# A convolution and a GRU on one core: x chunk 1 loaded behind the weights, candidate products by input part over a seeded bank, W_hh loaded gate by gate

## The chip, the core and the metric

The kernel runs on one core of one Trainium2 chip, in float32. The time is that of one execution on the device, in microseconds; the time of a kernel is the median of its runs. The profile is one more execution, recorded by the hardware profiler.

## The reference

The input x has 16 batch rows, 256 steps and 512 channels. First a causal depthwise convolution over time with 16 taps (the conditioning matrix gives one tap for each of its 16 rows), added to x. Then a GRU over the 256 steps, whose start state is the conditioning matrix, added to its own input:

```python
def _L0_cond_ref(x, w):                     # w: (16, 1, 512), K = 16
    return jax.lax.conv_general_dilated(x, w, window_strides=(1,), padding=[(K - 1, 0)],
        dimension_numbers=('NHC', 'HIO', 'NHC'), feature_group_count=C)

def cell(h, x):                             # W_ih, W_hh: (512, 1536); gates r, z, n
    gi = x @ W_ih + b_ih
    gh = h @ W_hh + b_hh
    i_r, i_z, i_n = jnp.split(gi, 3, axis=-1)
    h_r, h_z, h_n = jnp.split(gh, 3, axis=-1)
    r = jax.nn.sigmoid(i_r + h_r)
    z = jax.nn.sigmoid(i_z + h_z)
    n = jnp.tanh(i_n + r * h_n)
    h_new = (1.0 - z) * n + z * h
    return (h_new, h_new)

x = x + _L0_cond_ref(x, cond_2048[:, None, :])
x = x + _L1_cond_ref(cond_2048, x, W_ih, W_hh, b_ih, b_hh)
```

## The kernel before

**Layout.** The 512 channels lie on 128 partitions in four input parts, q (or kc) = 0 to 3. The 256 steps are cut into 16 chunks of 16 steps. A chunk of x arrives in `x_nat` by eight transfers (L125), VectorE transposes it into `xT` in two pieces (`turn`, L219), and the 16 steps before it are copied in front as a halo (ScalarE, L215). The convolved chunk is `x1T`. ScalarE makes the first term of each part (`first`, L236); the other 15 taps of each part are VectorE instructions that add to `x1T` in place (L257): 60 taps a chunk. `tap_units` gives their order: tap number k outside, part q inside.

**A step of the GRU** (`step`). TensorE multiplies the state with W_hh for r, then n, then z (`recurrent`, L409, 16 products each; the profile counts two instructions for one float32 product). The products add to PSUM banks that already hold the biases (`seed_rz` and `seed_nh`, copies on ScalarE) and, for r and z, the products of x with W_ih (`pair_units`, L374, a pair of steps at a time). The x part of the candidate comes from `ni_units` (L311): blocks of NI = 8 steps, for each output part q four input parts kc; when one q is complete it is evicted to SBUF with its bias added (L323), which makes four evictions a block. After sigmoid of r (ScalarE, L426), VectorE does `rn` (L435), its transpose (L437), `n` (L439), the transpose of z's products (L448), the difference `dn` (L454) and two halves of a scan that gives the new state (L461). `seen` (L389) is a copy of one element, a glance, with which VectorE takes note that ScalarE is done. Each engine runs its instructions in the order of the program, which is written by hand (`manual_schedule`).

**Work between.** `bulk_work` is called in each step after r's products are issued, and so lies on VectorE before `rn`. It draws one output unit (`out_units`: `sum` L497 or `store` L509, the sum and the transposition of 8 steps, two units in 8 steps) if one is due, then units of the `Plan`: taps, halos, transpositions. A unit has a cost (0.402 us a tap, 0.7 a transposition) and a due step. The quota of a step is `bulk.rate(t) + 0.175`, where `rate` is the greatest sum of costs up to a unit, divided by the steps left until it is due. Units are given while the sum plus half of the next cost is within the quota and the sum stays within ROOM = 2.05; a unit that is due in the next step is given in any case. Taps of chunk c were due 8 steps before the chunk begins. `other_products` gives, behind the step's own products on TensorE, up to two units of the next pair and two of the next candidate block.

**The start.** TensorE marks its banks (`mark`) and runs PAD tiny products to warm up. Chunk 0's parts 2 and 3 are convolved on TensorE with diagonal matrices (`conv_on_tensor`, L284; the diagonals from ScalarE, L280), parts 0 and 1 by taps on VectorE. Then the biases are spread by TensorE (`spread_biases`, L353), and the candidate's block 0 and the first pair are computed. Before step 0 the plan may give 10 us of chunk 1's taps (`bulk.run(0, HEAD)`, L582).

**Transfers.** SP and POOL issue the loads in the order of the program: the conditioning, x chunk 0, x chunk 1, the biases, then W_ih and W_hh in four transfers each (`load_weights`, L170, two on SP's queue, two on POOL's), then x chunk 2. A transfer on a queue waits until the one issued eight before it has landed.

Of the kernel before, what the change touches and what calls it, by code (L numbers as in the profile page):

```python
# [24 lines left out]
F32 = mybir.dt.float32  # L25
# [7 lines left out]
GT = 8  # L33
R, Z, N = 0, 1, 2
CHUNKS = (16,) * 16
PAD = 111
HEAD = 10.0
SYNC = mybir.DependencyInfo(mybir.DependencyClass.Sync, mybir.DependencyReason.DATA)
Q_PE = (2, 3)
NI = 8  # L40
# [35 lines left out]
def conv_gru_kernel(  # L76
# [29 lines left out]
    op = ctx.enter_context(tc.tile_pool(name="op", bufs=3))  # L106
    dram = ctx.enter_context(tc.tile_pool(name="dram", bufs=1, space=bass.MemoryType.DRAM))
    ps = ctx.enter_context(tc.tile_pool(name="ps", bufs=1, space=PSUM))
    ps_ni = ctx.enter_context(tc.tile_pool(name="ps_ni", bufs=2, space=PSUM))

    ctx.enter_context(tc.manual_schedule())

# [20 lines left out]

    warm = const.tile([P, 1], F32)
    nc.vector.memset(warm, 0.0)
    blank = const.tile([P, 2 * P], BF16)
    nc.vector.memset(blank, 0.0)
    for j in range(NQ):
        (nc.sync, nc.scalar)[j % 2].dma_start(
# [11 lines left out]
    nc.vector.memset(ones, 1.0)  # L151
    bn_nat = const.tile([P, P], F32)
    nc.vector.memset(bn_nat, 0.0)

    load_x(1, ((nc.sync,), (nc.gpsimd,)))
    nc.sync.dma_start(out=b_two[0:1, :], in_=b_hh.rearrange("(o c) -> o c", o=1))
    nc.sync.dma_start(
        out=b_two[1:2, 0 : 2 * C], in_=b_ih[0 : 2 * C].rearrange("(o c) -> o c", o=1)
# [5 lines left out]
    wih = const.tile([P, NQ, 3 * C], F32)  # L164
    whh = const.tile([P, NQ, 3 * C], F32)

    def load_weights(w_sb, w):

        for j in (0, 2, 1, 3):
            (nc.sync if j < 2 else nc.gpsimd).dma_start(  # L170
                out=w_sb[L * j : L * j + L],
                in_=w[j * P : (j + 1) * P].rearrange("(q l) c -> l q c", l=L),
            )

    load_weights(wih, w_ih)
    load_weights(whh, w_hh)
    load_x(2)
    zero_z = [const.tile([P, NQ * B * 2], F32, name=f"zero_z_{i}") for i in range(2)]
    for t in zero_z:
# [8 lines left out]
        nc.vector.tensor_scalar_add(last1, condT[:, :, K - 1], 1.0)  # L188

    bnT = const.tile([P, NQ, L], F32)  # L190

    b_rows = const.tile([P, 3, P], F32)

# [52 lines left out]
    def give_firsts(most=99):  # L246
        for _ in range(min(most, len(firsts))):
            firsts.pop(0)[2]()

    def tap_units(c):  # L250

        n = CHUNKS[c] * B

        def tap(k, q):
            while any(item[:2] == (c, q) for item in firsts):
                firsts.pop(0)[2]()
            nc.vector.scalar_tensor_tensor(  # L257
                out=x1T[c][:, q, 0:n],
                in0=xT[c][:, q, k * B : k * B + n],
                scalar=condT[:, q, k : k + 1],  # L260
                in1=x1T[c][:, q, 0:n],
                op0=ALU.mult,
                op1=ALU.add,
            )

        return [
            (0.135 + n / 960.0, lambda k=k, q=q: tap(k, q)) for k in range(K - 1) for q in range(NQ)
        ]

    def conv_on_tensor():  # L270

        n = CHUNKS[0] * B
        diag = const.tile([P, len(Q_PE), K, P], F32)

        def weight(k, q):
            return condT[:, q, k : k + 1] if k < K - 1 else last1[:, q : q + 1]

        for i, q in enumerate(Q_PE):
            for k in range(K):
                nc.scalar.activation(diag[:, i, k], ident, AF.Copy, scale=weight(k, q))  # L280
        for i, q in enumerate(Q_PE):
            acc = ps_ni.tile([P, CHUNKS[0] * B], F32, tag="pni", name=f"conv_{q}")
            for k in range(K):
                nc.tensor.matmul(  # L284
                    acc[:, 0:n],
                    lhsT=diag[:, i, k],
                    rhs=xT[0][:, q, k * B : k * B + n],
                    start=(k == 0),
                    stop=(k == K - 1),
                )  # L290
            evictions.append(lambda q=q, acc=acc: nc.scalar.copy(x1T[0][:, q, 0:n], acc[:, 0:n]))


    blocks = [(t0, NI) for t0 in range(0, T, NI)]

    def ni_units(t0, steps):

        n = steps * B
        c, o = chunk_of(t0)
        units = []  # L300
        hold = {}

        def prod(q, kc):
            if q == 0 and kc == 0:
                hold["ni"] = nip.tile([P, NQ, NI * B], F32, tag="ni", name=f"ni_{t0}")
                for i in range(steps):
                    ni[t0 + i] = hold["ni"][:, :, i * B : (i + 1) * B]
            if kc == 0:
                hold[q] = ps_ni.tile([P, NI * B], F32, tag="pni", name=f"pni_{t0}_{q}")
            for j in range(NQ):  # L310
                nc.tensor.matmul(  # L311
                    hold[q][32 * j : 32 * j + 32, 0:n],
                    lhsT=wih[:, kc, N * C + j * P + q * L : N * C + j * P + q * L + L],
                    rhs=x1T[c][:, kc, o : o + n],
                    start=(kc == 0),
                    stop=(kc == NQ - 1),
                    skip_group_check=True,
                )
            if kc == NQ - 1:
                evictions.append(lambda: evict(q))  # L320

        def evict(q):
            nc.scalar.activation(  # L323
                hold["ni"][:, q, 0:n], hold[q][:, 0:n], AF.Identity, bias=bnT[:, q, 0:1]
            )

        for q in range(NQ):
            for kc in range(NQ):
                units.append(lambda q=q, kc=kc: prod(q, kc))
        return units  # L330

    rz = [ps.tile([P, 2, P], F32, name=f"prz_{i}") for i in range(2)]
    nh = [ps.tile([P, P], F32, name=f"pnh_{i}") for i in range(2)]
    spare = ps.tile([P, 3, P], F32, name="spare")

    def mark():

        for i in range(2):  # L340
            nc.tensor.matmul(rz[i], lhsT=blank[:, 0:P], rhs=blank, start=True, stop=True)
            nc.tensor.matmul(nh[i], lhsT=blank[:, 0:P], rhs=blank[:, 0:P], start=True, stop=True)

    def idle_products(n):

        for _ in range(n):
            nc.tensor.matmul(
                spare[0:L, 0, 0:1], lhsT=blank[:, 0:L], rhs=blank[:, 0:1], start=True, stop=True
            )

    def spread_biases():
        for j in range(NQ):
            nc.tensor.matmul(  # L353
                spare[L * j : L * j + L],
                lhsT=ones,
                rhs=b_two.rearrange("o (g j c) -> o j g c", g=3, j=NQ)[:, j],
                start=True,
                stop=True,
            )

    def seed_rz(p):
        nc.scalar.copy(rz[p % 2], b_rows[:, 0:N])  # L362

    def seed_nh(p):
        nc.scalar.copy(nh[p % 2], b_rows[:, N])
# [28 lines left out]
    def step(t, h, bulk_work, other_products):  # L394
# [34 lines left out]
            tc.add_manual_dep(of_r.ins, of_z[-1].ins.name, SYNC, reason="its own earlier writes")  # L429
        if p + 1 < T // 2:  # L430
            (seed_nh if s else seed_rz)(p + 1)
        recurrent(pnh, N)
        seen(r, 0)
        rn = ew.tile([P, P], F32, tag="rn", name=f"rn_{t}")
# [91 lines left out]
    bulk = Plan()  # L526
    mark()
    idle_products(PAD)
    nc.tensor.drain()
    (_, halo), *turns = turn_units(0)  # L530
    halo()
    for t in hist:
# [12 lines left out]
            )  # L545
    conv_on_tensor()
    for i, (_, fn) in enumerate(tap_units(0)):
        if i % NQ not in Q_PE:
            fn()
    nc.vector.transpose(bnT, by_part(bn_nat))  # L550
    for _, fn in turn_units(1):
        fn()
    evictions.pop(0)()
    first_terms(1)
    give_firsts()
    evictions.pop(0)()
    spread_biases()
    nc.scalar.copy(b_rows, spare)
    seed_rz(0)
    seed_nh(0)  # L560
    for fn in ni_units(*blocks[0]):
        while evictions:
            evictions.pop(0)()
        fn()
    while evictions:
        evictions.pop(0)()
    for fn in pair_units(0):
        fn()
    for c in range(1, NCH):
        due = starts[c] - NI  # L570
        taps = tap_units(c)

        ahead = []
        if c + 1 < NCH:
            ahead = turn_units(c + 1) + [(0.0, lambda c=c: first_terms(c + 1))]
        at = len(taps) - AHEAD
        for cost, fn in taps[:at] + (ahead if c > 1 else []) + taps[at:]:
            bulk.add(cost, due, fn)
        if c == 1:
            for cost, fn in ahead:  # L580
                bulk.add(cost, due + GT // 2, fn)
    bulk.run(0, HEAD)  # L582

    h = (lambda kc: condT[:, kc, 0:B], condT[:, :, 0:B])
    late = []
# [1 line left out]
    for t in range(T):  # L587
        p, s = divmod(t, 2)
        if s == 0 and p + 1 < T // 2:
            of_pair = pair_units(p + 1)  # L590
        if t % NI == 0 and t + NI < T:
            of_block = ni_units(*blocks[t // NI + 1])

        def other_products():

            for units in (of_pair, of_block):
                for _ in range(2):
                    if units:
                        units.pop(0)()

        def bulk_work():

            quota = bulk.rate(t) + 2 * 0.7 / GT
            room = ROOM
            while late and (t >= T - 2 or room == ROOM):
                cost, fn = late.pop(0)
                fn()
                quota -= cost
                room -= cost
            bulk.run(t, quota, room)  # L610

        h = step(t, h, bulk_work, other_products)
        if t == T - 3:
            late += out_units(NG - 1, 0, GP - 1)
        elif t % GT == GT - 1 and t < T - 1:
            late += out_units(t // GT)
        elif t == T - 2:
            late += out_units(NG - 1, GP - 1, GP, (0,))
# [30 lines left out]
```

## Time and profile before

| | |
|---|---|
| runs | 1045.07, 1047.57, 1050.63 us |
| median | 1047.57 us |
| the profiled execution, its own time | 1048.66 us |
| its span, first to last instruction | 1046.7 us |
| busy: TensorE, its weight loads, VectorE, ScalarE | 98%, 88%, 88%, 36% of the span |
| first product of step 0 | 36.87 us |
| first product of step 1 | 42.09 us |
| W_ih landed (first, last of four) | 16.9, 24.1 us |
| W_hh landed (first, last of four) | 28.4, 36.4 us |

In the views of the profile a row names the engine, the line, the operation, the tile written and the tiles read, and the shape. PE is TensorE, PEld its weight load, DVE VectorE, ACT ScalarE, POOL GpSimd, SP the queue that issues transfers. "x5" means that five instructions in a row are merged into one row; the length then runs from the start of the first to the end of the last. In square brackets stands how long the engine sat idle before, and what ended that.

### The profile page before, as it was taken

The page shows a single profiled execution, that of the slowest core. Times are in us where ns is not written, and L with a number is a line of the kernel's source. Part 1 is how long each engine was busy: PE and PEld are TensorE (multiplying, and loading weights), DVE is VectorE, ACT ScalarE, POOL GpSimd, SP SyncE. Part 2 cuts the span into 40 slices and gives each one's busy share as a digit, 9 for nine tenths or more (in the row PEclk, how much of TensorE's full clock was granted, in tenths as well). Part 3 has the DMA queues.
Part 4 walks back from the last instruction along what each step waited for, and adds up shares of the span by engine and source line. Part 5 has one row for each costly group of instructions (what it writes and reads, how often), then busy time and mean ns, then how long its engine had stood idle before and what let it go on. Part 6 is the DMA issues. An engine that isn't in the chain of part 4 may idle for free.

```text
span 1046.7 us, 71583 instructions
## 1 busy us (share of the span) xinstructions
PE 1027.5 (98%) x32955; PEld 919.2 (88%) x32955; DVE 923.5 (88%) x3351; ACT 381.8 (36%) x1520; POOL 8.1 (1%) x21
## 2 busy tenths in 40 slices
PE   7799999999999999999999999999999999999997
PEld 6689989988989988988988988988888988988986
DVE  7899999999999998999999999998999999896555
ACT  5243433334333343333334333343333334333332
POOL 3000000000000000000000000000000000000000
PEclk9999999999999999999999999999999999999999
DMA  9510100101010010100100010010000000000000
GB/s 213 133 28 11 35 15 14 35 12 27 15 29 19 15 33 6 35 15 14 35 13 25 15 32 17 14 33 7 14 15 14 15 13 6 14 14 15 14 13 15
DMA packets 39760, 27.70 MB, mean 26 GB/s; under 512 B 6494, under 2 KB 38306, under 8 KB 39460
## 3 DMA queue, kind: packets, MB, share of 16 engines
q1 hardware_dynamic: 38180, 19.30, 8.4%
q8 instruction: 257, 4.21, 1.7%
q0 software_dynamic: 864, 3.67, 1.5%
q14 instruction: 43, 0.35, 0.1%
q10 hardware_dynamic: 416, 0.16, 0.1%
HBM read 14.73 MB, written 8.39 MB: 22 GB/s over the span
## 4 chain that ended last, share of the span: by engine, by line
PE 94%; DMA 3%; DVE 1%; ACT 0%; issue 0%; SPq 0%; ACTq 0%
PE prz L409 42%; PE pnh L409 21%; PE prz L374 20%; PE pni L311 10%; DMA whh<-in_L_cond_W_hh_dram 3%; DMA x_nat<-in_x_dram 0%; DVE rnT L437 0%; DVE rn L435 0%; DVE zp L448 0%; DVE n L439 0%; ACT zero_z L452 0%; DVE hist L461 0%; SPq L170 0%; DMA out_dram<-o 0%; DVE glance L389 0%
## 5 line engine op out<-in xcount | busy, mean ns | idle before, releaser
L409 PE MATMUL prz<-whh,hist 128*32 128x128 f32 x16320 | 539.2, 273 | 2.6 <-DVE hist L461 2.4
L409 PEld LDWEIGHTS prz<-whh,hist 128*32 128x32 f32 x16320 | 434.0, 103 | 19.5 <-DVE hist L461 5.8
L257 DVE SCALAR_TENSOR_TENSOR x1T<-xT,condT,x1T 128x256 f32<-128x256 f32 x930 | 381.0, 464 | 1.2 <-ACT x1T L236 1.2
L409 PE MATMUL pnh<-whh,hist 128*32 128x128 f32 x8160 | 269.5, 273 | 0.0
L374 PE MATMUL prz<-wih,x1T 128*32 128x256 f32 x4096 | 267.7, 379 | 0.0
L409 PEld LDWEIGHTS pnh<-whh,hist 128*32 128x32 f32 x8160 | 226.4, 104 | 0.0
L446 ACT ACTIVATE dn<-n 128x64 f32<-128x64 f32 x256 | 68.0, 266 | 322.2 <-DVE n L439 322.2
L374 PEld LDWEIGHTS prz<-wih,x1T 128*32 128x32 f32 x4096 | 127.7, 110 | 44.2
L311 PEld LDWEIGHTS pni<-x1T,wih 128*32 128x32 f32 x4096 | 122.1, 110 | 43.2 <-ACT x1T L236 0.6
L426 ACT ACTIVATE r<-prz 128x128 f32<-128x128 f32 x256 | 70.9, 277 | 243.2 <-PE prz L409 240.4
L311 PE MATMUL pni<-x1T,wih 128*32 128x128 f32 x4096 | 157.4, 273 | 0.0
L461 DVE TENSOR_TENSOR_SCAN hist<-zero_z,dn 128x64 f32<-128x64 f32 x512 | 115.4, 261 | 0.0
L435 DVE TENSOR_TENSOR rn<-r,pnh 128x128 f32<-128x128 f32 x256 | 72.8, 284 | 45.7 <-PE pnh L409 42.9
L452 ACT ACTIVATE zero_z<-zp 128x32 f32<-128x32 f32 x512 | 90.7, 226 | 7.6 <-DVE zp L448 0.2
L437 DVE STREAM_TRANSPOSE rnT<-rn 128x128 f32<-128x128 f32 x256 | 79.7, 311 | 8.8
L448 DVE STREAM_TRANSPOSE zp<-prz 128x128 f32<-128x128 f32 x256 | 81.1, 317 | 0.2
L323 ACT ACTIVATE ni<-pni,bnT 128x128 f32<-128x128 f32 x128 | 47.0, 367 | 75.1 <-PE pni L311 75.1
L454 DVE TENSOR_TENSOR dn<-hist,dn 128x64 f32<-128x64 f32 x255 | 58.2, 228 | 9.5
L439 DVE TENSOR_TENSOR n<-rnT,ni 128x64 f32<-128x64 f32 x256 | 57.6, 225 | 8.9
L389 DVE COPY glance<-r 1x1 f32<-1x1 f32 x256 | 34.1, 133 | 29.8 <-ACT r L426 29.6
L362 ACT COPY prz<-b_rows 128x256 f32<-128x256 f32 x128 | 48.6, 379 | 0.0
L389 DVE COPY glance<-zero_z 1x1 f32<-1x1 f32 x256 | 36.3, 142 | 8.9 <-ACT zero_z L452 0.2
(51 smaller groups left out, 216.3 us busy)
## 6 DMA issues: line engine op xcount, KB each, us to landing
out_dram<-o SPq DMA_DIRECT2D x248, 32.0 KB, 2.7
x_nat<-in_x_dram SPq DMA_DIRECT2D x118, 64.0 KB, 3.3
wih<-in_L_cond_W_ih_dram POOLq DMA_DIRECT2D x2, 768.0 KB, 12.8
wih<-in_L_cond_W_ih_dram SPq DMA_DIRECT2D x2, 768.0 KB, 13.9
whh<-in_L_cond_W_hh_dram POOLq DMA_DIRECT2D x2, 768.0 KB, 22.4
whh<-in_L_cond_W_hh_dram SPq DMA_DIRECT2D x2, 768.0 KB, 24.5
x_nat<-in_x_dram POOLq DMA_DIRECT2D x8, 64.0 KB, 5.5
out_dram<-o SPq DMA_DIRECT2D x8, 24.0 KB, 1.6
```

What stands on the lines that cost most here:

```text
L257: nc.vector.scalar_tensor_tensor(out=x1T[c][:, q, 0:n], in0=xT[c][:, q, k * B : k * B + n], scalar=condT[:, q, k : k + 1], in1=x1T[c][:, q ...
L311: nc.tensor.matmul(hold[q][32 * j : 32 * j + 32, 0:n], lhsT=wih[:, kc, N * C + j * P + q * L : N * C + j * P + q * L + L], rhs=x1T[c][:, k ...
L374: nc.tensor.matmul(rz[p % 2][32 * j : 32 * j + 32], lhsT=x1T[c][:, kc, o : o + PAIR], rhs=w_rz[:, :, j * P : (j + 1) * P], start=False, st ...
L389: nc.vector.tensor_copy(glances[i][0:1], of_scalar[0:1, 0:1])
L409: product = nc.tensor.matmul(dst[32 * j : 32 * j + m], lhsT=h[0](kc), rhs=whh[:, kc, g * C + j * P : g * C + (j + 1) * P], start=False, st ...
L426: of_r = nc.scalar.activation(r, pr, AF.Sigmoid)
L435: nc.vector.tensor_mul(rn, r, pnh)
L437: nc.vector.transpose(rnT, by_part(rn))
L446: nc.scalar.activation(dn_v[:, :, :, 1], n, AF.Tanh)
L448: nc.vector.transpose(zp, by_part(pz))
L452: nc.scalar.activation(z_v[:, qs, :, 1], zp[:, qs, half], AF.Sigmoid) for qs in halves
L461: nc.vector.tensor_tensor_scan(hist_g[:, lo + at : lo + at + W // 2], z[:, to], dn[:, to], 0.0, op0=ALU.mult, op1=ALU.add,)
```

## The change

- **Loads.** W_hh comes in twelve transfers, r first, then n, then z, each a 128-row quarter and 512 columns. x chunk 1 comes behind them.
- **Candidate products.** They go by input part: for each kc all four q. A block has one bank of 512 columns (`pni`), which ScalarE fills with the bias beforehand (`seed_ni`, from `bn_rows`); two evictions of 256 columns follow. The convolution of chunk 0 uses two `spare` banks, the first of which `spread_biases` writes later.
- **Taps.** Part q is now outside, tap number k inside, for chunk 0 as well. The taps of part i of chunk c are due at its first step - 7 + 2i.
- **Plan.** Chunk 1's transposition and first terms move from the start into the plan. Nothing is given before step 1 (FIRST). The next chunk's transposition stays 10 taps before the end of a chunk's taps, except for chunk 2, behind all taps of chunk 1.
- **Start.** 108 warming products in place of 111, two more marking products, no drain.

```diff
@@ -33,8 +33,8 @@
 GT = 8
 R, Z, N = 0, 1, 2
 CHUNKS = (16,) * 16
-PAD = 111
-HEAD = 10.0
+PAD = 108
+FIRST = 1
 SYNC = mybir.DependencyInfo(mybir.DependencyClass.Sync, mybir.DependencyReason.DATA)
 Q_PE = (2, 3)
 NI = 8
@@ -106,7 +106,6 @@
     op = ctx.enter_context(tc.tile_pool(name="op", bufs=3))
     dram = ctx.enter_context(tc.tile_pool(name="dram", bufs=1, space=bass.MemoryType.DRAM))
     ps = ctx.enter_context(tc.tile_pool(name="ps", bufs=1, space=PSUM))
-    ps_ni = ctx.enter_context(tc.tile_pool(name="ps_ni", bufs=2, space=PSUM))
 
     ctx.enter_context(tc.manual_schedule())
 
@@ -133,7 +132,7 @@
 
     warm = const.tile([P, 1], F32)
     nc.vector.memset(warm, 0.0)
-    blank = const.tile([P, 2 * P], BF16)
+    blank = const.tile([P, 4 * P], BF16)
     nc.vector.memset(blank, 0.0)
     for j in range(NQ):
         (nc.sync, nc.scalar)[j % 2].dma_start(
@@ -151,8 +150,6 @@
     nc.vector.memset(ones, 1.0)
     bn_nat = const.tile([P, P], F32)
     nc.vector.memset(bn_nat, 0.0)
-
-    load_x(1, ((nc.sync,), (nc.gpsimd,)))
     nc.sync.dma_start(out=b_two[0:1, :], in_=b_hh.rearrange("(o c) -> o c", o=1))
     nc.sync.dma_start(
         out=b_two[1:2, 0 : 2 * C], in_=b_ih[0 : 2 * C].rearrange("(o c) -> o c", o=1)
@@ -164,16 +161,18 @@
     wih = const.tile([P, NQ, 3 * C], F32)
     whh = const.tile([P, NQ, 3 * C], F32)
 
-    def load_weights(w_sb, w):
+    def load_weights(w_sb, w, columns):
 
         for j in (0, 2, 1, 3):
             (nc.sync if j < 2 else nc.gpsimd).dma_start(
-                out=w_sb[L * j : L * j + L],
-                in_=w[j * P : (j + 1) * P].rearrange("(q l) c -> l q c", l=L),
-            )
-
-    load_weights(wih, w_ih)
-    load_weights(whh, w_hh)
+                out=w_sb[L * j : L * j + L, :, columns],
+                in_=w[j * P : (j + 1) * P, columns].rearrange("(q l) c -> l q c", l=L),
+            )
+
+    load_weights(wih, w_ih, slice(0, 3 * C))
+    for g in (R, N, Z):
+        load_weights(whh, w_hh, slice(g * C, (g + 1) * C))
+    load_x(1, ((nc.sync,), (nc.gpsimd,)))
     load_x(2)
     zero_z = [const.tile([P, NQ * B * 2], F32, name=f"zero_z_{i}") for i in range(2)]
     for t in zero_z:
@@ -188,6 +187,7 @@
         nc.vector.tensor_scalar_add(last1, condT[:, :, K - 1], 1.0)
 
     bnT = const.tile([P, NQ, L], F32)
+    bn_rows = const.tile([P, NQ, NI * B], F32)
 
     b_rows = const.tile([P, 3, P], F32)
 
@@ -264,7 +264,7 @@
             )
 
         return [
-            (0.135 + n / 960.0, lambda k=k, q=q: tap(k, q)) for k in range(K - 1) for q in range(NQ)
+            (0.135 + n / 960.0, lambda k=k, q=q: tap(k, q)) for q in range(NQ) for k in range(K - 1)
         ]
 
     def conv_on_tensor():
@@ -279,79 +279,72 @@
             for k in range(K):
                 nc.scalar.activation(diag[:, i, k], ident, AF.Copy, scale=weight(k, q))
         for i, q in enumerate(Q_PE):
-            acc = ps_ni.tile([P, CHUNKS[0] * B], F32, tag="pni", name=f"conv_{q}")
+            acc = spare[i][:, 0:n]
             for k in range(K):
                 nc.tensor.matmul(
-                    acc[:, 0:n],
+                    acc,
                     lhsT=diag[:, i, k],
                     rhs=xT[0][:, q, k * B : k * B + n],
                     start=(k == 0),
                     stop=(k == K - 1),
                 )
-            evictions.append(lambda q=q, acc=acc: nc.scalar.copy(x1T[0][:, q, 0:n], acc[:, 0:n]))
-
-
-    blocks = [(t0, NI) for t0 in range(0, T, NI)]
-
-    def ni_units(t0, steps):
-
-        n = steps * B
+            evictions.append(lambda q=q, acc=acc: nc.scalar.copy(x1T[0][:, q, 0:n], acc))
+
+    def ni_units(t0):
+
+        b = t0 // NI
         c, o = chunk_of(t0)
-        units = []
         hold = {}
 
-        def prod(q, kc):
-            if q == 0 and kc == 0:
-                hold["ni"] = nip.tile([P, NQ, NI * B], F32, tag="ni", name=f"ni_{t0}")
-                for i in range(steps):
-                    ni[t0 + i] = hold["ni"][:, :, i * B : (i + 1) * B]
-            if kc == 0:
-                hold[q] = ps_ni.tile([P, NI * B], F32, tag="pni", name=f"pni_{t0}_{q}")
+        def prod(kc, q):
             for j in range(NQ):
                 nc.tensor.matmul(
-                    hold[q][32 * j : 32 * j + 32, 0:n],
+                    pni[b % 2][32 * j : 32 * j + 32, q],
                     lhsT=wih[:, kc, N * C + j * P + q * L : N * C + j * P + q * L + L],
-                    rhs=x1T[c][:, kc, o : o + n],
-                    start=(kc == 0),
+                    rhs=x1T[c][:, kc, o : o + NI * B],
+                    start=False,
                     stop=(kc == NQ - 1),
                     skip_group_check=True,
                 )
-            if kc == NQ - 1:
-                evictions.append(lambda: evict(q))
-
-        def evict(q):
-            nc.scalar.activation(
-                hold["ni"][:, q, 0:n], hold[q][:, 0:n], AF.Identity, bias=bnT[:, q, 0:1]
-            )
-
-        for q in range(NQ):
-            for kc in range(NQ):
-                units.append(lambda q=q, kc=kc: prod(q, kc))
-        return units
+            if kc == NQ - 1 and q % 2:
+                evictions.append(lambda: evict(slice(q - 1, q + 1)))
+
+        def evict(qs):
+            if qs.start == 0:
+                hold["ni"] = nip.tile([P, NQ, NI * B], F32, tag="ni", name=f"ni_{t0}")
+                for i in range(NI):
+                    ni[t0 + i] = hold["ni"][:, :, i * B : (i + 1) * B]
+            nc.scalar.copy(hold["ni"][:, qs], pni[b % 2][:, qs])
+
+        return [lambda kc=kc, q=q: prod(kc, q) for kc in range(NQ) for q in range(NQ)]
 
 
 
     rz = [ps.tile([P, 2, P], F32, name=f"prz_{i}") for i in range(2)]
     nh = [ps.tile([P, P], F32, name=f"pnh_{i}") for i in range(2)]
-    spare = ps.tile([P, 3, P], F32, name="spare")
+    pni = [ps.tile([P, NQ, NI * B], F32, name=f"pni_{i}") for i in range(2)]
+    spare = [ps.tile([P, NQ * P], F32, name=f"spare_{i}") for i in range(2)]
 
     def mark():
 
         for i in range(2):
-            nc.tensor.matmul(rz[i], lhsT=blank[:, 0:P], rhs=blank, start=True, stop=True)
+            nc.tensor.matmul(
+                rz[i], lhsT=blank[:, 0:P], rhs=blank[:, 0 : 2 * P], start=True, stop=True
+            )
             nc.tensor.matmul(nh[i], lhsT=blank[:, 0:P], rhs=blank[:, 0:P], start=True, stop=True)
+            nc.tensor.matmul(pni[i], lhsT=blank[:, 0:P], rhs=blank, start=True, stop=True)
 
     def idle_products(n):
 
         for _ in range(n):
             nc.tensor.matmul(
-                spare[0:L, 0, 0:1], lhsT=blank[:, 0:L], rhs=blank[:, 0:1], start=True, stop=True
+                spare[0][0:L, 0:1], lhsT=blank[:, 0:L], rhs=blank[:, 0:1], start=True, stop=True
             )
 
     def spread_biases():
         for j in range(NQ):
             nc.tensor.matmul(
-                spare[L * j : L * j + L],
+                spare[0][L * j : L * j + L, 0 : 3 * P],
                 lhsT=ones,
                 rhs=b_two.rearrange("o (g j c) -> o j g c", g=3, j=NQ)[:, j],
                 start=True,
@@ -360,6 +353,9 @@
 
     def seed_rz(p):
         nc.scalar.copy(rz[p % 2], b_rows[:, 0:N])
+
+    def seed_ni(b):
+        nc.scalar.copy(pni[b % 2], bn_rows)
 
     def seed_nh(p):
         nc.scalar.copy(nh[p % 2], b_rows[:, N])
@@ -429,6 +425,8 @@
             tc.add_manual_dep(of_r.ins, of_z[-1].ins.name, SYNC, reason="its own earlier writes")
         if p + 1 < T // 2:
             (seed_nh if s else seed_rz)(p + 1)
+        if t % NI == NI // 2 and t // NI + 2 < T // NI:
+            seed_ni(t // NI + 2)
         recurrent(pnh, N)
         seen(r, 0)
         rn = ew.tile([P, P], F32, tag="rn", name=f"rn_{t}")
@@ -526,7 +524,6 @@
     bulk = Plan()
     mark()
     idle_products(PAD)
-    nc.tensor.drain()
     (_, halo), *turns = turn_units(0)
     halo()
     for t in hist:
@@ -545,41 +542,43 @@
             )
     conv_on_tensor()
     for i, (_, fn) in enumerate(tap_units(0)):
-        if i % NQ not in Q_PE:
+        if i // (K - 1) not in Q_PE:
             fn()
     nc.vector.transpose(bnT, by_part(bn_nat))
-    for _, fn in turn_units(1):
-        fn()
+    nc.vector.tensor_copy(bn_rows, bnT[:, :, 0:1].broadcast_to([P, NQ, NI * B]))
+    for i in range(2):
+        seed_ni(i)
     evictions.pop(0)()
-    first_terms(1)
-    give_firsts()
     evictions.pop(0)()
     spread_biases()
-    nc.scalar.copy(b_rows, spare)
+    nc.scalar.copy(b_rows, spare[0][:, 0 : 3 * P].rearrange("p (g c) -> p g c", g=3))
     seed_rz(0)
     seed_nh(0)
-    for fn in ni_units(*blocks[0]):
-        while evictions:
-            evictions.pop(0)()
+    for fn in ni_units(0):
         fn()
     while evictions:
         evictions.pop(0)()
     for fn in pair_units(0):
         fn()
+
+    def ready(c):
+        return turn_units(c) + [(0.0, lambda: first_terms(c))]
+
+    for cost, fn in ready(1):
+        bulk.add(cost, starts[1] - NI, fn)
     for c in range(1, NCH):
-        due = starts[c] - NI
         taps = tap_units(c)
 
-        ahead = []
-        if c + 1 < NCH:
-            ahead = turn_units(c + 1) + [(0.0, lambda c=c: first_terms(c + 1))]
-        at = len(taps) - AHEAD
-        for cost, fn in taps[:at] + (ahead if c > 1 else []) + taps[at:]:
-            bulk.add(cost, due, fn)
-        if c == 1:
-            for cost, fn in ahead:
-                bulk.add(cost, due + GT // 2, fn)
-    bulk.run(0, HEAD)
+        at = len(taps) - (AHEAD if c > 1 else 0)
+        for i, (cost, fn) in enumerate(taps):
+            if i == at and c + 1 < NCH:
+                for unit in ready(c + 1):
+                    bulk.add(unit[0], starts[c], unit[1])
+
+            bulk.add(cost, starts[c] - NI + 1 + 2 * (i // (K - 1)), fn)
+        if at == len(taps):
+            for unit in ready(c + 1):
+                bulk.add(unit[0], starts[c], unit[1])
 
     h = (lambda kc: condT[:, kc, 0:B], condT[:, :, 0:B])
     late = []
@@ -589,7 +588,7 @@
         if s == 0 and p + 1 < T // 2:
             of_pair = pair_units(p + 1)
         if t % NI == 0 and t + NI < T:
-            of_block = ni_units(*blocks[t // NI + 1])
+            of_block = ni_units(t + NI)
 
         def other_products():
 
@@ -607,7 +606,8 @@
                 fn()
                 quota -= cost
                 room -= cost
-            bulk.run(t, quota, room)
+            if t >= FIRST:
+                bulk.run(t, quota, room)
 
         h = step(t, h, bulk_work, other_products)
         if t == T - 3:
```

## The prediction

> **What bounds the kernel now.** I read the chain of waits first, then the timeline of two steps, then the groups.
>
> In the chain, the columns are start, length (us) and what held it:
>
> ```profile
> 7.12 0.33 SPq L170
> ...
> 8.90 27.54 DMA whh<-in_L_cond_W_hh_dram
> 36.44 0.44 issue
> 36.87 1.91 PE prz L409 x32
> 38.78 1.29 PE pnh L409 x32
> 40.07 0.87 PE prz L409 x32
> ...
> 50.30 0.87 PE prz L409 x32
> 51.17 0.87 PE pnh L409 x32
> 52.04 0.87 PE prz L409 x32
> 52.91 0.86 PE prz L374 x16
> 53.78 0.44 PE pni L311 x16
> ```
>
> Until 36.4 us the program waits for W_hh. Step 0 then pays for a TensorE that has cooled (1.91 and 1.29 us where a warm one takes 0.87 each, 1.46 us in all). After that a step is 3 x 0.87 + 0.86 + 0.44 = 3.91 us of TensorE without a gap. Step 1 begins at 42.09, step 255 at 1038.58: 996.5 / 254 = 3.923 us a step, so all later stalls together are about 1 us. There is nothing to win behind the start, and 5 to 10 us before it.
>
> VectorE in one step with five taps, and the end of one with four (start, length):
>
> ```profile
> 50.13 2.03 DVE L257 SCALAR_TENSOR_TENSOR x1T<-xT,condT,x1T 128x256 f32<-128x256 f32 x5
> ...
> 52.09 0.14 DVE L389 COPY glance<-r 1x1 f32<-1x1 f32 x1
> 52.15 0.27 DVE L435 TENSOR_TENSOR rn<-r,pnh 128x128 f32<-128x128 f32 x1
> 52.45 0.31 DVE L437 STREAM_TRANSPOSE rnT<-rn 128x128 f32<-128x128 f32 x1
> 52.80 0.22 DVE L439 TENSOR_TENSOR n<-rnT,ni 128x64 f32<-128x64 f32 x1
> ...
> 57.97 1.64 DVE L257 SCALAR_TENSOR_TENSOR x1T<-xT,condT,x1T 128x256 f32<-128x256 f32 x4
> 59.54 0.13 DVE L389 COPY glance<-r 1x1 f32<-1x1 f32 x1
> 59.95 0.29 DVE L435 TENSOR_TENSOR rn<-r,pnh 128x128 f32<-128x128 f32 x1 [0.28 <-PE pnh L409]
> ```
>
> With four taps VectorE waits 0.28 us for TensorE before `rn`; with five it goes from the last tap straight into `rn`. So five taps are all that fits; what they last longer comes out of the recurrence, one for one. Second: a tap lasts 0.447 to 0.467 us, but taps start 2.03 - 1.64 = 0.39 us apart (0.396 over the 30 of the start). Neighbours overlap by 0.07 us. They can, because in the old order neighbours write different parts q. `rn`, `rnT`, `n` each read what the one before wrote, and each starts only 0.03 to 0.04 us after its end.
>
> **The change, part by part.**
>
> *Order of the taps.* From input part inside tap to tap inside input part: each tap now adds to what the tap just before it wrote. By the `rn`-`rnT`-`n` row it starts 0.034 us after that one's end: 0.447 + 0.034 = 0.48 to 0.466 + 0.034 = 0.50 us from start to start, 0.51 in the start phase (taps of 0.472 to 0.477 there). I take 0.49 against 0.396. From below the bound is 0.396, nothing; from above some 0.53.
>
> A rule of the Trainium skill speaks against me. "VectorE: DVE Perf Modes", section "The DRAIN you can't avoid", has every VectorE instruction wait until the pipe of the one before is empty, and eight copies lasting the same 13.88 us with a semaphore after each as with one at the end. By that rule the order costs nothing and the sum below is 1043. The row decides: 0.39 between starts of 0.466 us instructions is no empty pipe, and the same section concedes that an instruction that isn't held starts earlier.
>
> How many steps does it hit? The planner counts 0.402 us a tap and knows nothing of this. A fifth tap is given when the quota reaches 4 x 0.402 + 0.201 = 1.81. Working `rate` through the new deadlines: steps 2 to 7 and 10 to 13 get five (chunk 1 has to be done by step 14 from nothing, quota 1.85 to 2.02); then 18, 19, 26, 29; then three in each 16 steps (34, 42, 45, and so on, quotas 1.83, 1.98, 1.98) for twelve chunks; one at 234. That is 51, as against 35 before. Each runs 4 x (0.49 - 0.396) = 0.376 us longer, less about 0.04 us of slack: 0.34. 51 x 0.34 = 17 us. The 113 steps with four taps take 3 x 0.49 + 0.396 = 1.87 us, under the 1.98 of five old ones: free. Those with an output unit (0.61) or transpose (0.63) and three taps come to 1.99 to 2.01: free within 1 us in total. At 0.48 the whole is 14, at 0.50 19, at 0.52 25 us, by the same count.
>
> *The start.* x chunk 1 (four transfers on SP, 0.43 us each to issue, four on POOL at 0.53) goes behind the weights; W_hh has six issues on each queue in place of two. So W_ih is issued at about 3.5 us, not 7.12, behind 0.55 MB rather than 1.08. In the windows of the trace 512-byte runs move at 180 GB/s, 6 KB runs at 273. W_hh's runs become 2 KB: bounded by these two; by size nearer the upper, 250. Weights from 6 us: W_ih 11.5, then 4.2 a gate; with 1.6 us to land (as the 8 KB cond transfers) R is there at 23.3, N 27.5, Z 31.7, x chunk 1 at 34.6. At 180 GB/s Z lands at 37.
>
> But the weights stop being last. Preparation is, and it gets longer. x chunk 0 lands perhaps 0.6 us earlier; VectorE's 30 taps, in two runs of 15, take 15.2 us instead of 12.0 and end at 24.7. Then bias transpose and the broadcast `bn_rows` (512 elements; the 512-element transposes take 0.66) until 25.5; two seeds of [128x512] on ScalarE (copies of 128, 256, 384 columns take 0.27, 0.38, 0.48, hence 0.59 each) until 26.7; the eviction of part 2, queued behind the seeds, until 27.1. Now `spread_biases` writes the bank that held this convolution, so it waits for that eviction, and candidate products, gate products and step 0 are queued behind it on TensorE. Old lengths: spread 0.65, candidate 3.46, gates 1.73: step 0 starts at 32.95 with R and N present, asks for Z at 34.7 (landed 3 us before), and step 1 begins at 36.9 instead of 42.1. Gain 5.2 us, of which 1.46 is the cold TensorE.
>
> TensorE idles 24.1 to 27.1 here. "TensorE: Matmul & The Clock Gate", section "Part 1: The HAM clock gate", drops the clock after an idle window of about 3.4 us; the trace shows a drop within 5.6 idle us, costing 1.46. By the rule 3.0 us costs nothing and I take nothing; the other end is 1.5 us lost.
>
> *Chunk 1 inside the steps.* 25 taps ran under the wait for W_hh; that cover is gone, and they are in the count of 51. In step 1 ScalarE's first term waits behind two transposes and holds `r`: the old step 8 did just that and lost 0.7 us. That loss disappears; steps 1 and 15 get one each: +0.6 us. If x chunk 1 landed after 36.9, step 1 would wait for it in full, VectorE and ScalarE both; margin 2.3 us.
>
> *Moved without price.* On POOL `zero_z` now lies behind x chunk 1, whose last issue waits for the eighth transfer before it, a piece of R (23.3); it is needed at 35. Two more marking products (512 columns) fall into TensorE's 4.0 us wait for x; three warming products fewer and no drain: nil. Candidate products: same count, same shapes. Evictions: four of 0.367 per 8 steps become two of 0.38 plus a seed of 0.59, 1.35 against 1.47 us, on an engine busy 36%; the seed sits between `r` and `tanh`, which have 1.3 idle us there. Either way within 0.5 us.
>
> **The sum**, on the profiled run (1048.66 us, span 1046.7): -5.2 + 0.6 + 17 = +12.4, 1061.1. That run lies 1.1 above the median of the three, so I write 1060.
>
> **The rivals.**
> 1. As worked out (0.80): 1052 to 1072.
> 2. The taps' order is free, as the rule has it (0.09). Against it is the overlap in the row; for it, that a waiting semaphore might be signalled early. Preparation then ends at 30, step 0 waits for Z at 31.7 and step 1 begins at 35.5: -6.6 + 0.6 gives 1042. It decides below a spacing of 0.42.
> 3. Between (0.05), spacing 0.42 to 0.44: the taps take 2 to 7 us, cancelling the start; 1043 to 1052.
> 4. The wait costs more than 0.53 a tap (0.06): then the 113 four-tap steps no longer fit either, 0.06 us and more each; at 0.55 34 to 43 us, so 1077 to 1086.
>
> That the new load order doesn't reach the end is in case 1: Z lands 3 us before it is asked for, and only the part that preparation leaves is gained. Without any gain at the start: 1066.
>
> **How the numbers follow.** About 0.5% (5.2 us) is what a measurement here can tell from no change: faster is under 1042.3, slower over 1052.8. Case 2 gives 0.08 faster and 0.01 same; case 3 is mostly same; of case 1 a little lies at the edge. Faster 0.08, same 0.06, slower 0.86. The range 1050 to 1072 leaves out case 2, most of 3 and all of 4.
>
> **What would show it.** Right: L257 starts 0.48 to 0.51 apart within a part; five-tap steps of 4.3 us beside four-tap ones of 3.92; TensorE's idle time before L409 from `hist` near 17 us instead of 2.4; more of the chain on VectorE; first L409 near 33 with no wait on W_hh; a gap in TensorE before L353. Wrong: taps still 0.40 apart, or four-tap steps over 3.95, or a DMA ending the wait before step 0 or 1.

## The result, and the profile after

The changed kernel took 1077.04 us (median of four runs, 1075.21 to 1078.54), the kernel before 1047.79 beside it: 1.0278 times as long, 95% interval 1.0246 to 1.031. It is slower, as forecast, but outside the range that was given (1050 to 1072). The profiled execution took 1075.21 us with a span of 1073.3, 26.6 more than the span before.

From the pages of the two kernels, before and then after: the chain by engine, then two groups (busy time, mean ns of one | idle time before them, and what ended most of it):

```profile
PE 94%; DMA 3%; DVE 1%; ACT 0%; issue 0%; SPq 0%; ACTq 0%
...
L409 PE MATMUL prz<-whh,hist 128*32 128x128 f32 x16320 | 539.2, 273 | 2.6 <-DVE hist L461 2.4
...
L257 DVE SCALAR_TENSOR_TENSOR x1T<-xT,condT,x1T 128x256 f32<-128x256 f32 x930 | 381.0, 464 | 1.2 <-ACT x1T L236 1.2
```

```profile
DVE 56%; PE 34%; ACT 5%; issue 4%; DMA 1%; DVEq 0%; POOL 0%; SPq 0%; ACTq 0%; POOLq 0%
...
L405 PE MATMUL prz<-whh,hist 128*32 128x128 f32 x16320 | 541.3, 273 | 14.0 <-DVE hist L459 11.7
...
L257 DVE SCALAR_TENSOR_TENSOR x1T<-xT,condT,x1T 128x256 f32<-128x256 f32 x930 | 440.7, 477 | 24.6 <-ACT x1T L236 1.2
```

VectorE has taken over most of a chain that was TensorE's for 94%. The same 930 taps have 24.6 us of idle time in front of them, against 1.2 before, and only 1.2 of it is put down to ScalarE: the rest are gaps of some 35 ns between neighbours. TensorE's wait for the new state (`hist`) has grown from 2.4 to 11.7 us, less than the time that the steps have lost; their own lengths, below, carry the reading.

Two steps in the timeline of the changed kernel, one with five taps, one with a sum and three:

```profile
63.33 2.54 DVE L257 SCALAR_TENSOR_TENSOR x1T<-xT,condT,x1T 128x256 f32<-128x256 f32 x5
65.78 0.13 DVE L385 COPY glance<-r 1x1 f32<-1x1 f32 x1
65.85 0.27 DVE L433 TENSOR_TENSOR rn<-r,pnh 128x128 f32<-128x128 f32 x1
...
71.57 0.47 DVE L459 TENSOR_TENSOR_SCAN hist<-zero_z,dn 128x64 f32<-128x64 f32 x2
72.08 0.69 DVE L495 TENSOR_TENSOR sum<-x1T,hist 128x512 f32<-128x512 f32 x1
72.69 1.52 DVE L257 SCALAR_TENSOR_TENSOR x1T<-xT,condT,x1T 128x256 f32<-128x256 f32 x3
74.12 0.13 DVE L385 COPY glance<-r 1x1 f32<-1x1 f32 x1
```

Five taps hold VectorE for 2.54 us where they held it for 2.03, and `rn` follows at once. The median from start to start of neighbouring taps is 0.520 us over the whole trace; before it was 0.396.

Sorting the steps by what VectorE is given in them (time from one step's scan to the next) shows where the time sits. A step without a stall takes 3.918 us:

| in the step | before: count, mean us | after: count, mean us | over 3.918 us, after |
|---|---|---|---|
| five taps | 34, 3.924 | 51, 4.333 | 21.2 us in all |
| four taps | 114, 3.921 | 113, 3.919 | 0.1 |
| sum and three taps | 26, 3.921 | 28, 4.065 | 4.1 |
| store and three taps | 27, 3.929 | 29, 3.993 | 2.2 |
| the other steps | | | about 1.1 |

From the first scan to the last the steps took 1027.8 us, against 1000.4: +27.4. The start gave back next to nothing: step 0's scan came at 41.19 us instead of 41.77. Both together are the 26.6 us of the spans, but for 0.2 at the end.

The start in the chain of waits of the changed kernel (start, length):

```profile
10.48 0.49 DVE x1T L257
11.00 0.50 DVE x1T L257
...
25.68 0.68 DVE bn_rows L548
26.43 1.11 ACT pni L358 x2
27.89 0.85 PE spare L346 x8
28.74 5.30 PE pni L301 x128
34.04 1.73 PE prz L370 x32
35.97 1.62 issue
37.58 0.95 PE prz L405 x27
```

No transfer of W_hh is left in this chain. In its place stands a chain from VectorE's taps over the two seeds to TensorE, and in this two things that the prediction did not have: block 0 of the candidate takes 5.30 us, and TensorE stands for 1.62 us ("issue": it waited for nothing that the profile shows) inside step 0's products of r.

### The profile page after: what moved, and what is told of

Same layout as the page of the kernel before. It is cut to its first block, busy times and chain, and to the rows that moved or that the text cites. A ratio compares the mean times of both kernels' runs of the same rounds, so it can differ in the third digit from the quotient of the medians.

```text
span 1073.3 us, 71560 instructions
## 1 busy us (share of the span) xinstructions
PE 1045.4 (97%) x32954; PEld 920.6 (86%) x32954; DVE 956.9 (89%) x3352; ACT 371.5 (35%) x1488; POOL 10.3 (1%) x25
## 4 chain that ended last, share of the span: by engine, by line
DVE 56%; PE 34%; ACT 5%; issue 4%; DMA 1%; DVEq 0%; POOL 0%; SPq 0%; ACTq 0%; POOLq 0%
DVE x1T L257 26%; PE prz L405 16%; PE pnh L405 9%; PE prz L370 6%; DVE rnT L435 5%; DVE hist L459 5%; DVE n L437 4%; DVE rn L433 4%; PE pni L301 3%; ACT dn L444 3%; DVE glance L385 3%; DVE dn L452 2%; DVE o L507 2%; DVE sum L495 2%; DVE zp L446 2%
## 5 line engine op out<-in xcount | busy, mean ns | idle before, releaser
L405 PE MATMUL prz<-whh,hist 128*32 128x128 f32 x16320 | 541.3, 273 | 14.0 <-DVE hist L459 11.7
L257 DVE SCALAR_TENSOR_TENSOR x1T<-xT,condT,x1T 128x256 f32<-128x256 f32 x930 | 440.7, 477 | 24.6 <-ACT x1T L236 1.2
L433 DVE TENSOR_TENSOR rn<-r,pnh 128x128 f32<-128x128 f32 x256 | 69.8, 272 | 11.5 <-PE pnh L405 10.9
L317 ACT COPY ni<-pni 128x256 f32<-128x256 f32 x64 | 23.8, 373 | 39.7 <-PE pni L301 39.6
```

The source lines that it names most:

```text
L257: nc.vector.scalar_tensor_tensor(out=x1T[c][:, q, 0:n], in0=xT[c][:, q, k * B : k * B + n], scalar=condT[:, q, k : k + 1], in1=x1T[c][:, q ...
L405: product = nc.tensor.matmul(dst[32 * j : 32 * j + m], lhsT=h[0](kc), rhs=whh[:, kc, g * C + j * P : g * C + (j + 1) * P], start=False, st ...
L433: nc.vector.tensor_mul(rn, r, pnh)
```

## Experiments

**The order of the taps, undone in the changed kernel (e1_pairs).** The taps of parts 0 and 1 take turns, then those of 2 and 3. The due steps go with the pairs (first step of the chunk - 7 for one pair, - 3 for the other), and all else stays. The tails of chunks 1 and 2 stay part by part, to meet their due steps. "..." stands for lines left out.

```diff
...
+        part = [[(q, k) for k in range(K - 1)] for q in range(NQ)]
+        if c > 2:
+            return alternate(part[0], part[1]) + alternate(part[2], part[3])
+        return (
+            alternate(part[0], part[1])
+            + alternate(part[2][:7], part[3][:7])
+            + part[2][7:]
+            + part[3][7:]
+        )
...
-            (0.135 + n / 960.0, lambda k=k, q=q: tap(k, q)) for q in range(NQ) for k in range(K - 1)
-        ]
+        return [(0.135 + n / 960.0, lambda k=k, q=q: tap(k, q)) for q, k in tap_order(c)]
...
-            bulk.add(cost, starts[c] - NI + 1 + 2 * (i // (K - 1)), fn)
+            bulk.add(cost, starts[c] - NI + 1 + tap_due(c, i), fn)
```

> The changed kernel with one thing undone: the taps of parts 0 and 1 alternate, then those of parts 2 and 3, so that no tap adds to what the tap just before it wrote (only the tails of chunks 1 and 2 still do, about five steps). Theory A (taps that depend on their neighbour start 0.52 us apart and not 0.40): the steps go back to about 3.92 us, 25 us or more of the 28 us in the steps vanish, the start gains another 3 to 5 us because chunk 0's taps end near 22 us; total 1044 to 1050. Rival B (the loss in the steps comes from the seeded bank, the later due steps or the candidate products by input part): these are all kept, so at most the start moves and the total stays over 1068.

It took 1049.1 us, 1.0004 times the kernel before (0.999 to 1.0018). Its page, and two rows of its timeline:

```profile
L423 PE MATMUL prz<-whh,hist 128*32 128x128 f32 x16320 | 539.4, 273 | 3.7 <-DVE hist L477 3.1
L277 DVE SCALAR_TENSOR_TENSOR x1T<-xT,condT,x1T 128x256 f32<-128x256 f32 x930 | 383.3, 465 | 1.9 <-ACT x1T L236 1.2
```

```profile
53.84 2.03 DVE L277 SCALAR_TENSOR_TENSOR x1T<-xT,condT,x1T 128x256 f32<-128x256 f32 x5
55.80 0.14 DVE L403 COPY glance<-r 1x1 f32<-1x1 f32 x1
```

Five taps take 2.03 us again, the median distance is 0.396, and the steps take 1002.9 us instead of 1027.8, although 59 of them now have five taps. Over the pace of 3.918, 2.6 us are left in the five-tap steps; 22 taps of the tails still start about 0.52 us apart. One tap between two that depend on each other is enough. The seeded bank, the candidate's order and the later due steps (by pairs) are all still there and cost nothing that shows: rival B falls.

**The order of the taps alone, in the kernel before (e2_old_partfirst).**

```diff
-            (0.135 + n / 960.0, lambda k=k, q=q: tap(k, q)) for k in range(K - 1) for q in range(NQ)
+            (0.135 + n / 960.0, lambda k=k, q=q: tap(k, q)) for q in range(NQ) for k in range(K - 1)
...
-        if i % NQ not in Q_PE:
+        if i // (K - 1) not in Q_PE:
```

> The kernel before with the order of the taps alone changed to tap inside part. Theory A: by the classes of steps of the changed kernel, 35 five-tap steps x 0.415 us, 26 steps with a sum x 0.15, 27 with a store x 0.08, 26 with a transposition x 0.1 make 23 us; at the start the longer chunk 0 is hidden under the wait for W_hh: 1068 to 1073. Rival B: within 2 us of 1048.

1070.69 us, 1.0214 times the kernel before (1.0196 to 1.0231). Its 34 five-tap steps take 4.327 us, the steps with a sum 4.060, with a store 3.998: 13.9 + 3.7 + 2.2 us over the pace, and the steps are 19.4 us longer in all. The start lost another 2.7 us (first scan at 44.42), where it was thought hidden: the 25 taps given before step 0 now take 13 us and run into it. So this one part of the change lengthens the span by 22.1 us without the rest, against 26.6 for the whole change. From its page:

```profile
L257 DVE SCALAR_TENSOR_TENSOR x1T<-xT,condT,x1T 128x256 f32<-128x256 f32 x930 | 439.9, 477 | 24.4 <-ACT x1T L236 1.2
```

**The stop inside step 0 (e3_pad172).**

```diff
-PAD = 108
+PAD = 172
```

> The changed kernel with 172 warming products in place of 108, which shifts TensorE's place in its instruction stream by 128 instructions (half of a 16 KB piece). Theory C (the 1.6 to 2.0 us in which TensorE stands still inside step 0's first products, with no semaphore to wait for, is a late fetch of its instructions): the gap inside step 0 goes, or moves to another place of the start, and the time falls by 1 to 2 us to about 1075 to 1076. Rival D (it waits for W_hh or for ScalarE): the gap stays where it was, total 1077.

1073.38 us, a little under the forecast of 1075 to 1076; in the profiled run step 0's scan came 0.5 us earlier than in the changed kernel (40.66). TensorE in its timeline:

```profile
28.53 3.70 PE L301 MATMUL pni<-x1T,wih 128*32 128x128 f32 x128
32.05 1.91 PE L370 MATMUL prz<-wih,x1T 128*32 128x256 f32 x32
33.78 1.06 PE L405 MATMUL prz<-whh,condT 128*16 128x128 f32 x32
34.65 1.06 PE L405 MATMUL pnh<-whh,condT 128*16 128x128 f32 x32
38.78 1.07 PE L405 MATMUL prz<-whh,condT 128*16 128x128 f32 x32 [3.08 <-DMA x_nat<-in_x_dram]
```

The gap left the products of r and came back before those of z. The x transfer that the row names releases nothing that these products read, and Z's last quarter had landed by 36.5, 2.3 us before the gap ended.

TensorE's instructions come in pieces of 16 KB, about 256 to a piece. The page of the changed kernel lists 257 of them for 65,908 products and weight loads:

```profile
q8 instruction: 257, 4.21, 1.7%
```

Counted in the traces, the stop lies behind 694 to 698 instructions in four kernels (the changed one, e1_pairs, e4_old_by_gate, e5_warm) and, where 64 warming products are added in front, behind 948 in three (this one, e6_old_by_gate_pad, e7_pairs_pad): one piece later, as near as traces tell that miss a few records. In the seven kernels with W_hh by gate TensorE went on 2.8 to 3.1 us after the transfer of such a piece began: 34.54 to 37.58 in the changed kernel, 35.68 to 38.78 here, 30.79 to 33.58 in e1_pairs. That is theory C. The run also showed something not looked for: block 0 took 3.43 us from first to last start, on the same seeded bank.

**A warm TensorE (e5_warm).** 128 one-column products fill its idle time (3.00 us in the timeline of the changed kernel) before the biases are spread.

```diff
     conv_on_tensor()
+    for _ in range(128):
+        nc.tensor.matmul(
+            rz[1][0:L, 0, 0:1], lhsT=blank[:, 0:L], rhs=blank[:, 0:1], start=True, stop=True
+        )
```

> The changed kernel with 128 one-column products put on TensorE between the convolution and the spreading of the biases, where it sat idle for 3.4 us. They are 256 instructions, one whole 16 KB piece, so the place in the stream relative to the pieces is as before. Theory E (the candidate's block 0 took 5.3 us and not 3.46 because the clock fell to half at 29.8 us after that idle time): no record of half clock near 30 us, block 0 takes 3.4 to 3.5 us, step 0's products come 1.8 us earlier, about 1075. Rival (block 0 is slow because it accumulates on a seeded bank): still about 5.3 us, 1077.

1077.78 us: no gain. The timeline tells why:

```profile
25.36 3.35 PE L545 MATMUL prz<-blank 128*32 128x1 bf16 x128
28.64 0.85 PE L346 MATMUL spare<-b_two,ones 2*32 2x384 f32 x8
29.42 1.28 PE L301 MATMUL pni<-x1T,wih 128*32 128x128 f32 x35
34.59 4.13 PE L301 MATMUL pni<-x1T,wih 128*32 128x128 f32 x91 [3.90 <-issue]
```

The added instructions brought a piece border into block 0, and TensorE stood there for 3.9 us. The clock fell to half all the same, from 30.72 to 37.54: as the stop began, and so not because of it. The filling products did not keep the clock up, and the forecast (no half clock near 30 us, about 1075) missed on both counts. That block 0 is slow at half clock, and not because of its seeded bank, stands nevertheless, by e3_pad172 and by the clock of the changed kernel in its windows (the columns end with the granted clock, the DMA share and GB/s):

```profile
28.70:29.80 1.10, 1.10 (x46) 1.10 (x46) 0.00 (x0) 0.96 (x3) 0.00 (x0) 1.00 1.11 244
29.80:33.20 3.40, 3.40 (x76) 3.40 (x70) 0.00 (x0) 0.09 (x1) 0.00 (x0) 0.51 1.08 165
33.30:35.60 2.30, 2.30 (x61) 1.58 (x54) 0.00 (x0) 0.65 (x2) 0.00 (x0) 1.00 1.20 124
```

At full clock 46 of the products ran in 1.1 us, at half clock 76 in 3.4. Why the clock falls is taken up in the last section.

**The loads by gate alone, in the kernel before (e4_old_by_gate).**

```diff
...
-                out=w_sb[L * j : L * j + L],
-                in_=w[j * P : (j + 1) * P].rearrange("(q l) c -> l q c", l=L),
...
+                out=w_sb[L * j : L * j + L, :, columns],
+                in_=w[j * P : (j + 1) * P, columns].rearrange("(q l) c -> l q c", l=L),
...
-    load_weights(whh, w_hh)
+    load_weights(wih, w_ih, slice(0, 3 * C))
+    for g in (R, N, Z):
+        load_weights(whh, w_hh, slice(g * C, (g + 1) * C))
```

> The kernel before with W_hh loaded in twelve transfers gate by gate and nothing else. If the load order is worth what the prediction took it for: step 0's r products start near 31 us (R landed by 28, preparation done at 30.8) and z's as soon as Z lands near 36.5, so that step 1 starts 2.5 to 3.5 us earlier: 1044 to 1045.5. Rival: 2 KB runs slow the loads so that Z lands past 39, and nothing or less than 1 us is gained.

1046.17 us, 0.9974 times the kernel before (0.9965 to 0.9982): a gain of a quarter of a per cent, small but clear of the noise. From its chain of waits:

```profile
29.76 1.73 PE prz L375 x32
31.48 3.12 issue
34.60 1.91 PE prz L410 x32
36.51 1.40 PE pnh L410 x32
```

The wait for W_hh is gone, and 3.12 us in which TensorE waits for nothing that the profile shows are in its place, though R had landed at 28.5. Step 0's scan came 2.2 us earlier, less than forecast.

**The same with the piece border moved (e6_old_by_gate_pad, PAD = 175), and the control (e8_old_pad, PAD = 175 alone).**

> The kernel before with W_hh gate by gate, and 64 more warming products (175), half an instruction piece. With only the gates, step 0 began at 34.60 us though R had landed at 28.5 and the preparation ended at 31.3: TensorE stood for 3.1 us without a semaphore. Theory C (late instructions): step 0's first products start near 31.3, z's wait for Z at 36 to 37 instead, step 1 starts about 1 us earlier than with the gates alone: 1045. Rival: step 0 still starts at 34.6, 1046.2.

> Control: the kernel before with 175 warming products and nothing else. By theory C the late piece lies under the wait for W_hh (36.4 us) with either number, or moves into step 0: between no change and 1 us slower, 1047.5 to 1049. If the number of warming products mattered by itself (a warmer TensorE for the convolution), it would be faster by up to 1.5 us.

With the gates: 1046.51 us, 0.998 (0.997 to 0.9989). In the profiled run r's products start at 31.53 and the gap comes at the last product of n:

```profile
32.41 1.05 PE L410 MATMUL pnh<-whh,condT 128*16 128x128 f32 x31
36.30 0.28 PE L410 MATMUL pnh<-whh,condT 128*16 128x128 f32 x1 [2.85 <-issue]
```

Step 0's scan lies 1.2 us earlier than in e4_old_by_gate, but the runs scatter from 1044.05 to 1050.23 and their median is no better. The control (1049.28 us) is as fast as the kernel before: 1.0003 (0.9992 to 1.0014). The border moves as theory C says; a gain from moving it is not shown.

**Alternating pairs with the border moved (e7_pairs_pad).**

> The changed kernel with the taps in alternating pairs of parts and 172 warming products. Theory C: no gap before step 0's r products (30.5 us); the next piece is missing at z's products near 32 us, where Z has not landed before 34 anyway; step 1 starts at 36.5 to 37.2 instead of 37.5, 0.3 to 1 us faster than without the shift, so within 2 us under the kernel before. Rival: the start unchanged.

1048.58 us, 0.9998 (0.9988 to 1.0007), as without the shift. In the profiled run r's and n's products ran from 32.24 without a stop, then TensorE stood for 3.77 us before z's:

```profile
33.11 1.06 PE L423 MATMUL pnh<-whh,condT 128*16 128x128 f32 x32
37.94 1.07 PE L423 MATMUL prz<-whh,condT 128*16 128x128 f32 x32 [3.77 <-issue]
```

Step 1 began at 41.02, later than the 36.5 to 37.2 that were forecast. Z had landed by 36.7, so 1.3 us of the stop are the piece's alone.

## Why the prediction was right and wrong

**Right: the mechanism and its place.** A tap that adds to what its neighbour wrote starts after that one's end. The count was exact: 51 five-tap steps, and the 113 four-tap steps free (3.919 us). The row was right against the rule of the Trainium skill ("VectorE: DVE Perf Modes", section "The DRAIN you can't avoid"), which as the prediction read it makes the order of the taps free: e1_pairs and e2_old_partfirst put a price on the order, 0.520 against 0.396 us from start to start. The later due steps, seeds and evictions cost nothing that shows. R and N were there in time, and Z was not what ended a wait, though all came later than worked out: R at 24.9 us instead of 23.3, N at 29.4 instead of 27.5, Z at 35.3 instead of 31.7. A step 0 that began at 32.95 would have asked for Z 0.6 us too early.

**Wrong: the size of a tap.** The term was 0.49 us from start to start; it is 0.52 (a tap lasts 0.485 us, and the next starts 0.035 later). The 0.466 us of an overlapped tap was taken for the length of one that waits. A five-tap step costs 0.415 us and not 0.34: 21.2 us instead of 17. (Before, 34 steps had five taps, and not 35. By the prediction's own count 0.52 gives 51 x (4 x 0.124 - 0.04) = 23 us, and not 25; the measured steps had 0.08 us of slack.) The steps with an output unit and three taps were called free within 1 us; they cost 6.3. The sum starts 0.51 us after the scan that it reads began, where a free tap starts 0.38 after (72.08 and 71.57; 67.70 and 67.32): it depends on the scan, and that was not in the working. Against 17 + 1 us these two terms are about 9.5 us more.

**Wrong: the step "gain 5.2" at the start.** It came to 0.6 at step 0's scan, and 0.2 at step 1's first product (41.89 instead of 42.09; forecast 36.9). The 5.0 us between are in the timeline: the biases were spread at 27.89 and not 27.1 (0.8, mostly the taps); block 0 took 1.7 us longer, because the clock fell; 2.0 us were the stop at the piece border; step 0 itself was 0.4 longer. The prediction named the second as its other end (1.5) and put it at nothing, by the rule of the Trainium skill ("TensorE: Matmul & The Clock Gate", section "Part 1: The HAM clock gate") that it takes an idle window of about 3.4 us. The idle time was 3.00 us, as forecast, and the clock fell all the same (half from 29.85 to 33.26); the measurement decides. The length of one pause does not settle it, in either direction: see the last section. The stop at the border the prediction did not have at all: in the old profile a piece began at 30.67, and 3 us from there would lie unseen under the wait for W_hh, which lasted until 36.44.

Most of the gain at the start is there in e1_pairs, where the taps end in time and the clock stays full: step 1 began at 37.51 in its profiled run, 4.6 us before that of the old kernel. (For a preparation that ends in time, rival 2 had 35.5; the stop at the border, 2.71 us, is in between.) Yet its runs, from 1046.2 to 1052.0, have the median of the kernel before; the profiled one was the fastest of them. What differs in the slower ones is open; in e7_pairs_pad, where PAD alone differs, the start of the profiled run was 2.6 us longer (first scan at 39.82 against 37.19).

Of the rivals, 2 (order free), 3 (0.42 to 0.44) and 4 (over 0.53) are out. The spacing of 0.52 lay inside case 1, but not in the sum that was written for it.

Open, too, is why the piece of instructions comes so late. The 2.8 to 3.1 us hold with the DMA engines fully busy (e4_old_by_gate, 31.71 to 34.60) and about half busy (e3_pad172), so contention does not look like the cause; no kernel was made to tell. The faster version is e4_old_by_gate: the kernel before with W_hh by gate.

## What to carry to other kernels

On an engine that is full, look at what neighbouring instructions write: a chain of in-place updates cost a third more here than the same updates interleaved two by two (0.520 against 0.396 us each), and a planner that prices them alike won't see it. When a long wait is taken away, ask what it covered: here three things lay under it: a longer preparation, a TensorE clock that falls to half, and instructions that arrive late.

## What the runs showed of the hardware

**Late instructions.** TensorE stood still with no semaphore to wait for, at a border between two pieces of 256 instructions, and went on 2.8 to 3.1 us after the transfer of a 16 KB piece had begun. It was seen in the start alone (between 30.7 and 38.8 us); in the steps a piece comes about every 4 us without a stop.

**Dependent taps.** A dependent VectorE instruction is not merely held back: the same tap lasts 0.485 us with 0.035 between, against 0.466 with 0.070 of overlap.

**The granted clock.** In e2_old_partfirst TensorE waited 3.44 us for the first state and kept its full clock (a row of the timeline, and a window with the clock third from the end):

```profile
44.75 1.08 PE L409 MATMUL prz<-whh,hist 128*32 128x128 f32 x32 [3.44 <-DVE hist L461]
```

```profile
41.30:44.70 3.40, 0.01 (x2) 0.00 (x0) 3.09 (x13) 0.61 (x3) 0.00 (x0) 1.00 0.30 82
```

In e3_pad172 it kept it over 3.08 us; in the changed kernel it lost it 2.0 us behind a pause of 3.00, and in e2_old_partfirst, at 29.16, behind pauses of 0.97 and 1.74. What fits all ten traces is a grid. Within a trace, every change of the clock after it first became full lies a whole number of 3.413 us stretches behind that moment (the changed kernel: full at 12.78, half at 29.85, which is 5 stretches, full at 33.26, which is 6). A full clock fell at the end of each stretch in which TensorE had products for 1.28 us or less, and of none with 1.48 us or more. So a pause that lies across a border of the grid is shared out between two stretches.

For this the one-column products and the spreading of the biases (two rows deep) must be left out of the count, and that rests on two stretches: 1.18 us without and 1.95 with them in the changed kernel, 1.28 and 3.39 in e5_warm. It would explain why e5_warm's filling products did not help. The rule was read from the traces afterwards, and no kernel was made to test it.
